# Token maxima by VectorE's 32-squares and four small transfers per pair of sequences, paired gathers, and a new hand-written order

## The chip, the cores and the metric

The kernel runs on one core of a Trainium2 chip. The core has five engines that run side by side, each through its own list of instructions in order: TensorE (PE; its weight loads are shown as PEld), VectorE (DVE), ScalarE (ACT), GpSimd (POOL) and SyncE (SP), which here only issues DMA transfers. The engines wait for one another through semaphores. The metric is the device time in microseconds; a figure given as "the time" is the median of three runs. A profile is one separate execution with the hardware profiler on.

## The reference

Eight sequences x of 256 tokens by 128 features in float32 run through a block of this kind: a mixture-of-slots layer (soft MoE), linear attention with 16 heads, the same mixture-of-slots layer a second time, a gated feed-forward layer with ternary weights, random-feature attention (FAVOR), and the feed-forward layer again, each added to x. The change touches the mixture-of-slots layer:

```python
logits = einsum('bnd,esd->bnes', x, se)          # 256 tokens x 1024 slots per sequence
dispatch = softmax(logits, axis=1)               # over tokens
combine = softmax(logits.reshape(b, n, -1), -1)  # over all 1024 slots of a token
slots = einsum('bnd,bnes->besd', x, dispatch)
eout = expert_e(slots)                           # 16 experts, 64 slots each
out = einsum('bns,bso->bno', combine, eout)
```

The softmax of `combine` subtracts from each token's logits their maximum over all 1024 slots: the token maxima of the title.

## The kernel before

**Stages.** The eight sequences form two groups of four. Each group goes through two mixture layers (with linear attention, `linear`, between), a feed-forward stage (`glu`), FAVOR attention (`favor`) and a second `glu`. The functions of a stage only record steps: for each, the engines that could run it with a planned cost, what it reads and writes, and the buffers it takes. All are recorded first, then `Plan.place` puts them in the sequence of the tuple `ORDER`, a hand-made list of step numbers (a negative number takes a step's second possible engine), gives each a planned start, and hands out buffers of the pools in `kinds`. `Plan.issue` emits the steps sorted by planned start. So stages of different groups lie in between one another, and each engine's list is fixed by `ORDER`. Where a TensorE step that takes a new PSUM bank is planned to wait over 700 ns, `issue` puts filling products against the identity ahead of it (`idle`, line L1440 before and L1503 after), which keep TensorE's clock up and compute nothing.

**`dispatch(b, sl, late)`**, per sequence and layer: normalize x (`norm`; statistics on VectorE, the root on GpSimd), transpose it by identity products (`transposed`), write the normalized tokens to DRAM and read them back four times over, so that each group of 32 partitions holds all tokens (`replicated`). Then eight matmuls of logits (L670), 128 slots by 256 tokens each, copied from PSUM into the buffer `comb` (128 partitions x 8 x 256). A partition holds a slot of each of eight blocks. For the softmax over tokens, per half of `comb`: maxima (L701), exponentials with sums (L709), reciprocals (L717), a multiplication on GpSimd (L722) into `ex`, and a VectorE transposition of 32x32 squares (L730). The gather (`gathered`, L743) multiplies the squares with the replicated tokens in 32 matmuls on quarters of the array, and four evacuations with the affine scale (`affinely`, L560 or L562) put the slots into `sl`.

**The token maxima.** Within a partition, the maximum over the eight slot blocks is taken on VectorE: in the very first layer (`late`) in one reduction (L762), else while the logits are copied (L687) and by a last `fold` (L759). Then it has to go across the 128 partitions. Before the change:

```python
flip(pt.ap[:, t, :], pm.ap[:, 0, ts(t, P)])       # transpose by identity: tokens on partitions
nc.vector.tensor_reduce(mn.ap, pt.ap, AX.X, ALU.max)
flip(pb.ap[:, ts(t, P)], mn.ap[:, t : t + 1].to_broadcast([P, P]))  # back, on all partitions
```

`flip` is line L455 in the profile, the reduction L778; a copy from PSUM (`evacuated`, L460 or L462) gives `mb`. GpSimd subtracts `mb` from `comb` (L796) and ScalarE takes the exponentials (L802).

**`experts`** loads the weights of one expert after the other (L823, six buffers), multiplies (L837), applies GELU on ScalarE (L843) and the gate on VectorE (L848), multiplies again (L868), adds the bias (L874) and places the result by transfer (L881). **`combine`** (L910) multiplies the exponentials with the experts' results. In `glu`, L1193 and L1196 are the two gates, L1124 the hidden products, L1138 and L1109 their sums, L1146 the GELU and L1221 the last product. L519 and L525 are the transfers of another transposition through DRAM (`squares_turned`).

Of the kernel before, what the change touches and what calls it, by code (L numbers as in the profile page):

```python
# [9 lines left out]
F32 = mybir.dt.float32  # L10
# [3 lines left out]
P = 128  # L14

ORDER = (
    10, 11, 0, 37, 38, 3, 19, 20, 1, 2, 7, 8, 6, 4, 5, 13, 12, 40, 39, 41, 43, 53, 44, 42, 21, 22,
    23, 24, 14, 132, 133, -136, 172, 62, 63, 31, 134, 136, 137, 15, 16, 17, 18, 142, 140, 60, 9,
    143, 141, 32, 25, 26, -34, -35, 35, 36, 56, 1329, -28, 92, -29, 93, -96, -95, 98, 61, 173,
    1286, 1287, 148, -1290, 149, 29, -31, 68, 138, -1289, 146, 147, 57, 144, -146, 96, 97, 69,  # L20
    150, 66, 67, 64, 65, 163, 1292, 100, 73, -175, 104, 105, 70, 101, 102, 103, 106, 107, 164,
    139, -176, 176, 108, 1290, 177, 182, -1292, 180, 1294, 1330, -1332, -1333, 1333, 165, 166, 71,
    74, 178, 153, 109, 1334, 75, 76, 186, 187, 181, 184, 167, 72, 113, 114, 151, 183, 1345, 77,
    99, 154, 78, 82, 79, 80, 185, 81, 110, 1302, 1339, 51, 1295, 1337, 1338, 83, 115, 1342, 111,
    112, 116, 188, 155, 156, 117, 118, 193, 1335, 1336, 189, 1340, 152, 50, 1341, 190, 191, 194,
    119, 157, -123, 1343, 179, -121, 195, 1344, 1347, 121, 1346, 196, 192, 197, 158, 1299, 1348,
    160, 159, 162, 49, 161, 1349, 168, 48, 355, 203, 198, 200, -202, -200, 1372, 1296, 204, 1415,
    84, 85, 205, 202, 359, 366, 370, 1416, -1419, 1297, 1298, 1301, 1303, 360, 361, 356, 1304,
    357, 358, 1373, -1375, 250, 251, 252, 253, 1375, 1350, 1351, 254, 324, 325, 326, 1300, 328,
    334, 1353, 1376, 1377, 1310, 1305, 367, 379, 86, 368, 87, 88, 369, 206, -1418, 373, 338, 335,  # L30
    374, 219, 255, 256, 268, 90, 329, 371, 330, 372, 376, 327, 269, 1382, -208, 210, 341, 123,
    342, 1388, 339, 340, 336, 337, 1380, 1363, 1306, 1381, 170, 1384, 377, 220, 1307, 124, 125,
    -1390, 52, 345, 1385, 1354, 1355, 261, 223, 352, 353, 221, -1384, 224, 1387, 1378, 1356, 346,
    1386, 1320, 349, 350, 292, 293, 262, 225, 222, 347, 263, 1293, 1390, 1406, 236, 237, 296, 297,
    351, 1352, 265, 266, 281, 348, 264, 294, 1407, 1408, 240, 244, 1308, 241, 295, 242, 1409, 245,
    267, 47, 1357, 303, 298, 246, 304, 305, 306, 362, 363, 307, 308, 270, 1358, 243, 208, 209,
    1396, 310, 1421, 375, 1391, -1361, 378, 1311, 311, 278, 279, 1392, 1393, 1321, 1322, -1411,
    1411, 1312, 354, 257, 258, -1362, 1397, 271, 272, 1364, 273, 309, 274, 1365, 212, 213, 214,
    216, 275, 276, 229, 230, 231, 1398, 215, 233, 282, 1313, 286, 234, 235, 1362, 313, 217, 218,
    283, 317, 323, 1394, 1379, 232, 312, 287, 314, 1359, 364, 288, 238, 284, 277, 1419, 318, 319,  # L40
    285, 315, 316, 280, 1399, 1400, 1395, 259, 344, 1413, 1323, 1324, 169, 320, 321, 1420, 1366,
    343, 289, 290, 226, 227, 228, 91, -1368, 291, 1422, 126, 127, 130, 331, 131, 1309, 1412, 239,
    1370, 247, 1314, 248, 299, 1368, 332, 333, 1325, 260, 211, 1401, 1402, 171, 300, 1369, 249,
    1315, -1319, -1320, 301, 1316, 322, 1612, 1428, 1429, 1431, 1432, 89, 1538, -1404, 1439, 1423,
    1425, -1405, 1440, -1427, 1441, -1318, 365, 302, 1496, 459, 1424, 1434, 1427, 1435, 1436,
    1326, 381, 128, 45, 380, 382, 1442, 129, 1443, 433, 1437, 1528, 1438, 1327, 1430, 383, 384,
    432, 458, 434, 1517, 435, 1433, -386, 460, 461, 386, 1444, 1549, 1446, 436, 1448, 406, -1448,
    387, 1328, 388, -438, 407, 389, -439, 462, 463, 1405, 464, 1445, 1518, 408, 465, 1449, 439,
    1542, 1543, 1616, 1613, 1614, 409, 410, 412, 411, 1544, 1497, 1498, 1500, 1501, 1499, 1519,
    1520, 1539, 1540, 1617, 1521, 1529, 1550, 1551, 1553, 1541, 1615, 442, 1618, 440, 413, 1502,  # L50
    1514, 1530, 1554, 1555, 1552, 1515, 466, 1450, 1451, 1532, 1522, 1523, 441, 443, 445, 1452,
    1531, 391, 1533, 414, 1535, 416, 468, 1453, 1454, 1371, 1536, 467, 446, 1622, 1623, 444, 449,
    448, 469, 470, 1534, 1548, 1458, 474, 1456, 471, 472, 473, 1459, 392, 397, -397, 475, 1556,
    1566, 447, 393, 394, 395, 1507, 1567, 1537, 1511, 1512, 1513, 1508, 1509, 1510, 1460, 1461,
    1465, 1469, 1557, 390, 476, 477, 398, 1470, 1471, 46, 1466, 1467, 450, 415, 399, 417, 451,
    1468, 1601, 1414, 1569, 1591, 478, 400, 401, 1524, 1525, 479, 1545, 1546, 402, 419, 1462, 403,
    404, 405, 418, 422, 1568, 484, 485, 1475, 1516, 480, 420, 421, 1595, 423, 1596, 452, 453,
    1605, 1606, 1482, 1483, -488, 1547, 454, 1479, 1602, 486, 1597, -456, 1463, 1486, 1607, 1490,
    1558, 1464, 1603, -482, 456, 1604, 488, 457, 570, 571, 1487, 1488, 489, 573, 1472, 1473, 1476,
    1477, 482, 1478, 1625, 483, 613, 614, 1580, 1584, 1585, 1491, 54, 55, 1492, 492, 494, -494,  # L60
    496, 1506, -616, 497, -499, 495, 500, 501, -617, 617, 618, 424, 425, 1592, 426, 1581, 1611,
    1480, 1489, 499, -573, 1503, 1481, 1593, 1594, 502, 1582, 1583, 1457, 508, 574, 1608, 621,
    509, 626, 1609, 622, -576, 578, 1455, 427, 623, 503, 1504, 619, 629, 624, 518, 1559, 1563,
    510, -580, 1586, 1570, 1474, 490, 625, 491, 627, 628, 631, 632, 504, 505, 1527, 580, 1610,
    582, 583, 584, 511, 512, 1598, 1624, 1599, 1493, 1494, 1495, 519, 520, 630, 581, 1564, 1560,
    1561, 1562, 428, 1565, 506, 507, 1571, 1572, 429, 1619, 1620, 1485, 1574, 1575, 1576, 1577,
    430, 431, 527, 528, 1505, 1621, 633, 513, 1578, 1573, 1587, 529, 530, 531, 532, 637, 634, 635,
    638, 1484, -516, 1588, 589, 586, 537, -588, 585, 588, 535, 594, 540, 543, -545, 536, 541, 539,
    542, 514, 1579, 636, 1590, 1600, 1526, 1589, 1653, 639, 1652, 640, 521, 620, 576, 577, 1678,
    538, 546, 545, 551, 595, 596, 641, 1679, 597, 590, 591, 592, 552, 1680, 1654, 1655, 1656,  # L70
    -1658, 598, 1627, 553, 1626, 1628, 522, 547, 533, 548, -517, 517, 642, 644, 646, 593, 599,
    -1659, 643, 1659, -646, 549, 550, 554, 561, 555, 600, 534, 556, 559, 1629, 604, 558, 1660,
    -604, 1630, -1632, 1632, 557, 1662, 1705, 1633, 1681, 1682, -1685, 1704, 1706, 562, 563, 602,
    1707, 1708, 673, 799, -1684, 560, 601, 677, 678, 679, 1634, 674, 675, 803, 804, 805, 647, 800,
    810, 778, 782, 1661, -1710, 1710, 1711, 779, 1714, 726, 801, 802, 780, 1685, 676, 811, 812,
    648, 649, 684, 783, 784, 814, 815, 1664, -1669, 1669, 816, 813, 1635, 691, 688, 689, 820, 692,
    1637, 1639, 1638, 1712, 1686, 525, 821, 690, 781, 685, 686, 687, 1663, 1665, 1713, 1642, 1643,
    789, 1715, 1717, 564, -566, 1687, 1640, 1641, 701, 702, 796, 1644, 817, 1645, 1646, 1666,
    1667, 566, 567, 730, 797, 1647, 58, 1689, 1691, 1648, 1649, 1716, 1721, -1721, 818, 568, 1690,
    757, 1695, 1718, 1719, 1670, 1671, 523, 1692, 656, 660, -1695, 657, 1693, 1636, 1722, 1723,  # L80
    1672, 1673, 661, 727, 1724, 1725, 1688, 1650, 728, 729, 736, 1651, 790, 731, 732, 761, 650,
    651, 1696, 662, 1726, 1730, 743, 744, 762, 763, 1727, 663, 667, 791, 693, 1728, 1729, 668,
    669, 605, 1674, 1675, 704, 1731, 1697, -1734, 606, 793, -1733, 1734, 664, 683, 658, -1736,
    1859, 1860, 822, 1676, -1863, 1698, 1677, 1773, 1774, 652, 794, 795, 1699, 1746, 659, 792,
    1747, 1738, 1740, 1739, 1742, 1743, 1745, 665, 806, 705, 709, 1748, 703, 809, 666, 1700, 1701,
    807, 710, 737, 1744, 1754, 819, 607, 1741, 1749, 1702, 1703, 608, -1777, 738, 758, 759, 760,
    -1776, 706, -1862, 1865, 1863, -1865, 707, 740, 739, 680, 711, 681, 1869, 708, 741, 775, 776,
    654, 1867, 1750, 798, 1868, 768, 823, -1871, 1878, 1751, 1777, 569, 1779, 1875, 670, 671,
# [1436 lines left out]
```

## Time and profile before

| what | value |
|---|---|
| time, median of 3 (lowest to highest) | 718.74 us (718.47 to 719.14) |
| the profiled execution's own time | 720.09 us |
| its span, first to last instruction | 718.4 us |
| granted TensorE clock | 1.0 over the whole span |
| transfers | 72.76 MB, 36% of 16 engines' time on the queue of SyncE |

The page of a profile gives for each engine its busy time, its share of the span and its number of instructions; the chain of work that ended last, followed back from the end; and the costliest groups of instructions, as "line engine operation out<-in shapes xcount | busy us, mean ns of one | idle time ahead and what ended it". A matmul in float32 runs as two passes and counts as two instructions in the profile. Other views are answers of the trace: busy time by stretches of the span, what an engine waited for ("engine line waited <- releaser: us in total, times, longest"), the timeline of an engine, and the chain in order of time. An engine's line number is that of the kernel, so the same line has different numbers before and after.

### The profile page before, as it was taken

The numbers are of one execution on the slowest core, as the hardware profiler recorded it, in microseconds if no ns is written. First come the engines' busy times: TensorE is split into PE (matmuls) and PEld (weight loads), VectorE is DVE, ScalarE is ACT, GpSimd is POOL, SyncE is SP. The second block draws the span as 40 slices with busy tenths as digits, with TensorE's granted clock in tenths as the row PEclk, the third lists the DMA queues.
The fourth block names the chain that finished last, engine by engine and source line by source line (L and its number), as shares of the span: only waits on it lengthen the run. The fifth ranks groups of instructions, "written<-read, shape, count | busy, mean of one in ns | idle before, by whom it ended". The sixth has DMA issues, their size and how long they took to land.

```text
span 718.4 us, 14349 instructions
## 1 busy us (share of the span) xinstructions
PE 710.3 (99%) x5266; PEld 609.3 (85%) x5266; DVE 496.6 (69%) x1087; ACT 391.4 (54%) x780; POOL 326.6 (45%) x432
## 2 busy tenths in 40 slices
PE   8999999999999999999999999999999999999998
PEld 6889889998899999999788879876886878868787
DVE  7999774767997688974534545787576877875432
ACT  4987677464865547784642544566435542452421
POOL 6848377531327355745884321352425563413020
PEclk9999999999999999999999999999999999999999
DMA  4553566154344644462642321023404143241001
GB/s 134 162 201 99 165 160 225 34 157 124 118 113 134 182 133 127 120 195 90 203 137 67 84 67 43 18 61 89 73 16 89 44 92 58 59 90 30 12 11 37
DMA packets 118741, 72.76 MB, mean 101 GB/s; under 512 B 73360, under 2 KB 107536, under 8 KB 118672
## 3 DMA queue, kind: packets, MB, share of 16 engines
q1 hardware_dynamic: 118672, 71.85, 36.0%
q8 instruction: 42, 0.69, 0.4%
q14 instruction: 27, 0.22, 0.1%
HBM read 51.89 MB, written 11.53 MB: 88 GB/s over the span
## 4 chain that ended last, share of the span: by engine, by line
PE 95%; POOL 2%; DMA 1%; ACT 1%; DVE 1%; issue 0%; POOLq 0%; ACTq 0%
PE ps L1124 27%; PE ps L837 15%; PE ps L743 8%; PE ps L910 8%; PE ps L868 7%; PE ps L670 7%; PE ps L1221 4%; PE ps L1193 4%; PE ps L1196 4%; PE ps L455 2%; PE ps L1297 1%; PE ps L1347 1%; PE ps L1382 1%; PE ps L958 1%; DMA we<-in_We 1%; POOL sm L486 1%
## 5 line engine op out<-in xcount | busy, mean ns | idle before, releaser
L837 PE MATMUL ps<-slots,we 128*128 128x256 f32 x512 | 122.5, 380 | 1.8 <-ACT k L843 0.9
L837 PEld LDWEIGHTS ps<-slots,we 128*128 128x128 f32 x512 | 92.9, 190 | 14.8 <-ACT slots L560 1.2
L1124 PE MATMUL ps<-comb,comb 128*128 128x256 f32 x448 | 103.0, 380 | 0.0
L1124 PE MATMUL ps<-comb,slots 128*128 128x256 f32 x448 | 102.5, 380 | 0.0
L1124 PEld LDWEIGHTS ps<-comb,slots 128*128 128x128 f32 x448 | 84.1, 190 | 13.2 <-issue 1.8
L1124 PEld LDWEIGHTS ps<-comb,comb 128*128 128x128 f32 x448 | 83.6, 190 | 13.1 <-issue 1.7
L843 ACT ACTIVATE k<-ps,small 128x256 f32<-128x256 f32 x128 | 57.5, 475 | 60.1 <-PE ps L837 52.5
L796 POOL TENSOR_TENSOR comb<-comb,k 128x1024 f32<-128x1024 f32 x32 | 75.4, 2364 | 31.3 <-ACT k L460 8.8
L722 POOL TENSOR_TENSOR comb<-comb,sm 128x1024 f32<-128x1024 f32 x32 | 60.3, 1895 | 41.5 <-DVE sm L717 37.8
L848 DVE SCALAR_TENSOR_TENSOR k<-ps,small,k 128x256 f32<-128x256 f32 x128 | 57.4, 476 | 19.5 <-ACT k L843 18.2
L460 ACT COPY k<-ps 128x512 f32<-128x512 f32 (+2 forms) x52 | 25.6, 497 | 78.9 <-PE ps L1124 56.1
L868 PEld LDWEIGHTS ps<-we,k 128*128 128x128 f32 x512 | 63.6, 192 | 4.8 <-issue 2.0
L709 ACT ACTIVATE comb<-comb,sm 128x256 f32<-128x256 f32 x128 | 63.6, 507 | 4.6 <-DVE sm L701 2.4
L868 PE MATMUL ps<-we,k 128*128 128x128 f32 x512 | 65.7, 276 | 0.0
L484 POOL TENSOR_SCALAR sm<-sm 128x2 f32<-128x2 f32 x52 | 10.0, 193 | 121.7 <-DVE sm L478 112.1
L1138 DVE TENSOR_TENSOR comb<-ps,k 128x512 f32<-128x512 f32 x48 | 32.6, 686 | 47.1 <-PE ps L1124 35.3
L670 PE MATMUL ps<-k,seT 128*128 128x256 f32 x256 | 60.4, 383 | 0.8 <-ACT seT L596 0.4
L910 PEld LDWEIGHTS ps<-slots,comb 128*128 128x128 f32 x512 | 58.6, 192 | 1.3 <-issue 1.0
L910 PE MATMUL ps<-slots,comb 128*128 128x129 f32 x512 | 59.6, 276 | 0.0
L743 PE MATMUL ps<-comb,k 32*128 32x256 f32 x1024 | 59.5, 379 | 0.0
L1146 ACT ACTIVATE comb<-comb 128x512 f32<-128x512 f32 x48 | 29.3, 629 | 51.9 <-DVE comb L1138 51.8
L743 PEld LDWEIGHTS ps<-comb,k 32*128 32x128 f32 x1024 | 52.7, 185 | 4.5 <-ACT comb L460 0.3
(147 smaller groups left out, 1286.0 us busy)
## 6 DMA issues: line engine op xcount, KB each, us to landing
we<-in_We SPq DMA_DIRECT2D x64, 448.0 KB, 4.1
k<-y SPq DMA_DIRECT2D x64, 128.0 KB, 2.7
slots<-k SPq DMA_DIRECT2D x128, 64.0 KB, 2.1
t<-comb SPq DMA_DIRECT2D x8, 512.0 KB, 2.8
k<-t SPq DMA_DIRECT2D x32, 128.0 KB, 3.1
y<-k SPq DMA_DIRECT2D x16, 128.0 KB, 2.6
t<-k SPq DMA_DIRECT2D x16, 128.0 KB, 1.7
k<-t SPq DMA_DIRECT2D x64, 32.0 KB, 2.3
```

The costliest lines, as they stand in the source:

```text
L670: mm(pl.ap[:, j, :], seT[:, 2 * u + j].rearrange("p k s -> p (k s)"), yt.ap, start=True, stop=True,)
L709: nc.scalar.activation(ex.ap[:, 4 * h + j, :], comb.ap[:, 4 * h + j, :], AF.Exp, bias=mx.ap[:, j : j + 1], accum_out=mx.ap[:, 4 + j : 5 + j],)
L722: return nc.gpsimd.tensor_tensor(ex.ap[:, part], ex.ap[:, part], mx.ap[:, 8:12].unsqueeze(2).to_broadcast([P, 4, N]), ALU.mult,)
L743: mm(po.ap, yr.ap[rows, TT * (c % 4) + c // 4, :], ex.ap[rows, :, 32 * c : 32 * c + 32], start=(c == 0), stop=(c == N // 32 - 1), tile_pos ...
L796: return nc.gpsimd.tensor_tensor(raw, raw, mb.ap.unsqueeze(1).to_broadcast([P, 4, N]), ALU.subtract)
L837: mm(pe.ap[:, m, :], we.ap[:, ts(2 * m + c, P)], sl.ap[:, j, k, :, 0:S], start=True, stop=True,)
L843: nc.scalar.activation(ga.ap, pe.ap[:, 0, :], AF.Gelu, bias=bg[:, e, c : c + 1])
L848: nc.vector.scalar_tensor_tensor(ht.ap[:, c, :], pe.ap[:, 1, :], bu[:, e, c : c + 1], ga.ap, ALU.add, ALU.mult,)
L868: mm(po.ap[:, r, :], ht.ap[:, c, ts(r, P)], we.ap[:, ts(4 + c, P)], start=(c == 0), stop=(c == 1),)
L910: mm(po.ap[:, t, 0 : D + 1], comb.ap[:, j, ts(t, P)], eo()[:, j, q, 0 : D + 1], start=(j == 0), stop=(j == NJ - 1),)
L1124: mm(bank.ap[:, o], w(k)[:, c, ts(o, P)], rhs().rearrange("p (c n) -> p c n", c=2)[:, c, :], start=(start and o + c == 0), stop=(stop and ...
L1138: nc.vector.tensor_tensor(C(i, k)(), bank.ap.rearrange("p o n -> p (o n)"), other(), ALU.add)
```

## The change

`dispatch` now ends with the squares of `ex`. The gather is a function of its own and takes one or two sequences; with two, their results lie in one PSUM bank each and leave it in one evacuation of 512 columns. It takes two where the group and the layer have different numbers, one where they are equal. The token maxima are a third function, `maxima`, for two sequences always: VectorE transposes the 32x32 squares of the folded maxima and takes the maximum in each square, which leaves for each token four maxima, one for each 32 partitions; a transfer writes them to DRAM (`spill`), a second reads them back so that the four lie side by side on 32 partitions (`fetch`); VectorE takes their maximum and turns the square; a third transfer writes 512 maxima to DRAM (`give`), and a fourth reads them on all 128 partitions (`spread`). The identity products, the reduction from PSUM and the copy are gone. The pool of `comb` has ten buffers instead of nine, that of `k4` five instead of four, and the scratch memory for dynamic DMA is set to 2048 bytes. `plan.tag` is set in many places and only labels steps. `ORDER` is new throughout, so all engines' lists differ from the first instruction on.

```diff
     kinds = {
-        "comb": (NJ * N, 9),
+        "comb": (NJ * N, 10),
...
-        "k4": (1024, 4),
+        "k4": (1024, 5),
...
+        return comb, pm, ex, yr
+
+    def gather(b, got, sl):
+        n, q = len(got), b % BG
+        pos = [ps_(n, NJ, 32) for _ in range(4)]
         def gathered(_):
-            for c in range(N // 32):
-                for a, po in enumerate(pos):
...
+            for k, (_, _, ex, yr) in enumerate(got):
+                for c in range(N // 32):
+                    for a, po in enumerate(pos):
+                        rows = slice(32 * a, 32 * a + 32)
+                        mm(po.ap[:, k], yr.ap[rows, TT * (c % 4) + c // 4, :],
+                           ex.ap[rows, :, 32 * c : 32 * c + 32], ...)
...
+    def maxima(b, got, late):
+        n = len(got)
+        mb, mq = Buf("k2", (P, n, N)), Buf("sm", (P, 32))
+        K = n * N // 32
...
-        step({"PE": flips(TT)}, turn_max, [pm], [pt])
-        step({"DVE": dve(N)}, token_max, [pt], [mn])
...
-        step({"PE": flips(TT)}, spread, [mn], [pb], takes=[mb])
-        evacuated(lambda: mb.ap, lambda: pb.ap, [pb], [mb], N)
+        def quarters(_):
+            nc.vector.transpose(flat(), flat())
             nc.vector.tensor_reduce(
+                mq.ap[:, 0:K], flat().rearrange("p (k j) -> p k j", j=32), AX.X, ALU.max)
+        def spill(_):
+            nc.sync.dma_start(parts.rearrange("a i k -> (a i) k"), mq.ap[:, 0:K])
+        def fetch(_):
+            nc.sync.dma_start(flat()[0:32, 0 : 4 * K].rearrange("i (a k) -> i a k", a=4),
+                              parts.rearrange("a i k -> i a k"))
+        def tops_of(_):
+            four = flat()[0:32, 0 : 4 * K].rearrange("i (a k) -> i k a", a=4)
+            nc.vector.tensor_reduce(
+                mq.ap[0:32].rearrange("i (r k) -> i r k", k=K),
+                four.unsqueeze(1).to_broadcast([32, 32 // K, K, 4]), AX.X, ALU.max)
+            nc.vector.transpose(flat()[0:32, 4 * K : 4 * K + 32], mq.ap[0:32])
+        def give(_):
+            nc.sync.dma_start(whole, flat()[0:K, 4 * K : 4 * K + 32])
         def spread(_):
-            for t in range(TT):
-                flip(pb.ap[:, ts(t, P)], mn.ap[:, t : t + 1].to_broadcast([P, P]))
+            nc.sync.dma_start(flat(), whole.rearrange("k i -> (k i)").partition_broadcast(P))
...
+            first, single = g + layer == 0, g == layer
+            for b in bs_ if single else bs_[::2]:
+                got = []
+                for k in range(1 if single else 2):
+                    got.append(dispatch(b + k, sl, first))
+                if single:
+                    both.append((b, got[0]))
+                gather(b, got, sl)
+                if single and len(both) == 2:
+                    got = [z for _, z in both]
+                    b, both = both[0][0], []
+                if len(got) == 2:
+                    maxima(b, got, first)
```

## The prediction

> **What bounds the kernel now.** First the page: the busy share of each engine, and the engines' shares of the chain that ended last.
>
> ```profile
> PE 710.3 (99%) x5266; PEld 609.3 (85%) x5266; DVE 496.6 (69%) x1087; ACT 391.4 (54%) x780; POOL 326.6 (45%) x432
> ...
> PE 95%; POOL 2%; DMA 1%; ACT 1%; DVE 1%; issue 0%; POOLq 0%; ACTq 0%
> ```
>
> TensorE (PE) is busy 710.3 of 718.4 us and carries 95% of the chain. A busy share alone doesn't say that an engine is full. So, second, the busy time of TensorE in two stretches, cut where the experts' products begin (columns: stretch, its length, busy time), and, third, all that TensorE waits for after the cut.
>
> ```profile
> 0.00:52.50 52.50, 49.37 (x430) 1.00 0.54 170
> 52.50:718.40 665.90, 660.95 (x4838) 1.00 0.35 96
> ...
> PE ps L837 <- ACT k L843: 0.9, 1, 0.9
> PE ps L837 <- DMA we<-in_We: 0.6, 1, 0.6
> PE ps L837 <- DVE k L874: 0.3, 1, 0.3
> ```
>
> After 52.5 us it idles 4.95 us. Of this 3.1 are the tail behind its last product, which ends at 715.3; 1.85 are waits, in 663 us. There, a product taken from TensorE's list is worth the time it occupies, and work put on other engines costs nothing until something arrives late. The first 52 us differ. The timeline of TensorE, then of VectorE (DVE), shows why (start, length, instruction):
>
> ```profile
> 30.04 3.92 PE L743 MATMUL ps<-comb,k 32*128 32x256 f32 x64
> ...
> 28.62 1.25 DVE L730 STREAM_TRANSPOSE comb<-comb 128x1024 f32<-128x1024 f32 x1
> 47.55 3.77 DVE L762 TENSOR_REDUCE k<-comb 128x256 f32<-128x2048 f32 x1
> 51.30 0.99 DVE L562 TENSOR_SCALAR slots<-ps,small 128x256 f32<-128x256 f32 x2
> ```
>
> The first gather (L743) starts at 30.04, 0.17 us after the end of the VectorE transpose that it needs. The first expert product comes at 52.55, just after the last slots leave PSUM (52.29), and these stood behind a maximum of 3.77 us (L762). VectorE sets the pace there.
>
> **What is removed.** Per sequence and layer two transposes of maxima and two spreading products against the identity go: 4 x 16 = 64, from 144 identity products to 80. Two views give a price, that of the line's durations and the chain in order of time:
>
> ```profile
> L455 PE MATMUL ps<-ident,sm x32: 272/273/273, 27.1 to 342.6; 128*128 128x128 f32 x32
> ...
> 27.08 0.44 PE ps L455 x4
> ```
>
> Each lasts 273 ns, but four take 0.44 us of the chain, 0.11 each, because neighbours overlap. 64 x 0.11 = 7.0 us. The Trainium skill (TensorE: Matmul & The Clock Gate, Part 4: PE-mode transpose) puts one at about 275 ns in a kernel's context, which is this row's duration; priced so, the removal would be an estimated 17.6 us, and the spacing in the chain speaks against that.
>
> VectorE loses 16 reductions L778 of 0.41 us (6.6 us), ScalarE (ACT) 15 copies of 0.38 us (5.7 us). Hardly anything on TensorE waited for them: zero.
>
> **The gathers.** The same 512 matmuls remain; pairing saves the seam between two gathers. The chain again:
>
> ```profile
> 47.55 3.67 PE ps L743 x64
> ...
> 106.08 7.12 PE ps L743 x128
> ```
>
> Two in a row take 7.12, not 2 x 3.67: 0.22 us per seam. But the old order already has neighbours: its 16 gathers stand in 11 runs. The new order has 10. Gain 0.2 us. The evacuations fall from 64 to 48, the paired ones twice as wide; other stages' products follow each paired gather and cover them.
>
> **What is added on VectorE.** Per pair: a transpose of 512 columns (L516, 0.71 us); a maximum of 512 to 16 (nearest L1309, 0.68); a small maximum over 128 elements (between L611's 0.17 and L778's 0.41; I take 0.25); a transpose of one square (between 0.18 for the smallest statistics row and 0.44 for 256 columns; I take 0.2, as it is nearer in size). Together 1.84 us, for eight pairs 14.7, net of L778 8 us: from 69% to about 70%. Behind them in VectorE's queue stand evacuations, and TensorE waits for those. But after 52.5 us VectorE has 47 blocks of 1.2 us (L730, L701) and one of 3.77 in the same queue, and the waits are those shown. So zero, at 1.4 us for each block whose cover is gone. The skill (VectorE: DVE Perf Modes, Rules for kernel authors) speaks against the change: it sends a 128x128 transpose to TensorE where PSUM will do. By that rule the sum would have no gain and an estimated 8 us of extra VectorE work; the busy shares above say that here TensorE is the engine to spare.
>
> **What is added on SyncE (SP).** 32 transfers, per pair four in series: spill, fetch, give, spread. Nearest rows of the transfers (last number: us from issue to landing):
>
> ```profile
> t<-k SPq DMA_DIRECT2D x16, 128.0 KB, 1.7
> k<-t SPq DMA_DIRECT2D x64, 32.0 KB, 2.3
> k<-t SPq DMA_DIRECT2D x32, 128.0 KB, 3.1
> ```
>
> Four are between 6.8 and 12.4 us. The first three move 8 KB or less, the last writes 256 KB: I take 1.7 + 2.1 + 1.7 + 2.8 = 8.3. With VectorE's 1.84 the maxima take 10 us instead of about 2. The cover is the experts: the maxima serve GpSimd's (POOL) subtraction L796 (four of 2.36 us per pair), ScalarE's exponentials (1.06) and only then the combining product L910, behind all sixteen experts. A stage of experts is (122.5 + 65.7) / 4 = 47 us of TensorE by lines L837 and L868. 10 + 9.5 + 1 fits.
>
> Fetch and spread wait on SP for a landing, the experts' weights (L823) queued behind them. SP has taken such waits (L525 for its spill: 22.8 us over 16, 1.9 at most), and TensorE waited 0.6 us for weights in all. Zero; 1 to 3 us for each that breaks through.
>
> ScalarE's list has 71 table loads instead of 57: 14 x 1.28 = 18 us, less 5.7. Zero by the same argument, 1.28 for each that stands in front of an activation TensorE needs. Pools, scratch size and tags issue nothing.
>
> **The new start.** Up to the first expert product TensorE's list has 22 identity products instead of 28, the same logits and gathers, and 35 filling products instead of 25. VectorE's list now has two maxima L762 ahead of the first gather's last transpose, where one stood. The statistics block ends 1.1 us later (two more pairs, one more normalization); then come seven maxima L701 (1.1 each), two L762 (3.67), three reciprocals (0.08) and two transposes (1.14): 14.3 + 1.1 + 17.6 = 33.0. TensorE's list agrees: eight more logits (0.44 each) and two more fills, less four identity products, put 30.04 at 33.6. By VectorE the second gather is ready at 39.3 (L762, two transposes), the third at 43.4, the fourth at 48.7. A gather takes 3.67, so the fourth ends at 52.4; the slots take 1.4 more, as before: 53.8, or +1.25 us. Bounds: 0, if the early waits shrink; +3, if each of three gaps costs a further half microsecond.
>
> **Sum.** After the first expert product 116 identity products become 58: 58 x 0.11 = 6.4 less; the seam 0.2 less; the start 1.25 more. Net -5.35: the span goes from 718.4 to 713.05. The profiled execution's own time was 720.09, 1.69 over its span, so 714.74; it stood 1.35 over the median of 718.74, so the median goes to 713.4. The 1.85 us of waits I leave. They can go (-1.85) or, since every queue is ordered anew, grow: four more like the longest (0.9) are +3.6. So the forecast's own range is 711.5 to 717.0.
>
> **Rivals.** *The chain of transfers arrives late* (slower). Its weakest place is the last pair of the second group's second layer: its fetch stands 24 issues behind its spill on SP, eight fetches of hidden weights among them (4.4 to 4.7 us to landing), its spread another 24 on. If the cover is gone, the price is what the chain adds, 8 us: 721.4. It turns the sign once the last exponential ends over 5.3 us after TensorE is ready for that product. Against it: nine of the sixteen experts' placements still follow the spread, some 9 x 2.9 = 26 us of TensorE, for 2.8 + 9.5 + 1. *VectorE or ScalarE takes it back* (no change): 8 and 12 us more work, and a quarter of it (5 us) in front of evacuations gives 718.4. For it: the first 52 us, where VectorE is the bound. Against: from 130 to 230 us it is busy 80%, later less. *A denser order*: the waits go and the start costs nothing, 713.4 - 1.85 - 1.25 = 710.3. That nothing is removed is excluded: the instruction lists show the 64 gone.
>
> **Chances.** Forecast 0.72; denser order 0.05; no change, 717.0 to 720.2, 0.09, of which 0.01 still below 717.3; late chain, or a wait of that size elsewhere, 0.14. A measurement of this kernel tells 0.2%, 1.4 us, from no change: faster is below 717.3, slower above 720.2. Faster 0.78, same 0.08, slower 0.14. The range 711.0 to 720.0 leaves out the late chain and most of the denser order, under 0.2.
>
> **What would show it.** Right: about 7 us less identity work on TensorE and 2 us more fills; double gathers of 7.1 us; the first expert product near 53.8; waits of TensorE after it under 5 us; the spread landing long before L910. Wrong: TensorE waiting at L910 for ScalarE's exponentials (late chain), waits for evacuations over all stages (the engines), or a first expert product after 56.

## The result and the profile after

The changed kernel takes 721.05 us (median of 13 runs, 719.88 to 724.78), the kernel before 718.74 (13 runs, 717.71 to 719.83). The ratio is 1.0038, 95% interval 1.0027 to 1.0049: 2.7 us (1.9 to 3.5) slower. The forecast of 713.4 us and its range, 711.0 to 720.0, missed it. The profiled execution took 722.52 us, 1.47 over the median. Differences of two experiments below are taken from their ratios to the kernel before, times 718.7 us; their error is the two half intervals added in squares.

The page after, with the lines shown of before:

```profile
PE 707.7 (98%) x5222; PEld 607.4 (84%) x5222; DVE 504.3 (70%) x1098; ACT 394.6 (55%) x755; POOL 335.9 (47%) x444
...
PE 77%; DVE 8%; DMA 6%; SPq 3%; ACT 3%; POOL 1%; issue 1%; DVEq 0%; ACTq 0%
```

TensorE is 2.6 us less busy in a span 2.4 us longer, and its share of the chain falls from 95% to 77%: VectorE, transfers and SP's own queue (SPq) now stand in it. Where, the stretches tell, cut at the first expert product and at the first combining product (length, then each engine's busy time, clock, share of the DMA engines, GB/s). After:

```profile
0.00:54.80 54.80, 50.72 (x444) 43.94 (x445) 48.82 (x92) 41.12 (x119) 33.75 (x68) 1.00 0.50 152
54.80:118.70 63.90, 59.45 (x420) 52.61 (x418) 47.93 (x97) 42.64 (x97) 36.74 (x29) 0.97 0.55 147
118.70:720.80 602.10, 597.51 (x4360) 510.87 (x4360) 407.52 (x910) 310.89 (x542) 265.41 (x347) 1.00 0.36 95
```

Before, cut at the same two products:

```profile
52.50:116.70 64.20, 63.34 (x507) 56.34 (x506) 49.24 (x100) 47.95 (x103) 43.04 (x35) 1.00 0.49 136
116.70:718.40 601.70, 597.61 (x4333) 511.15 (x4331) 400.59 (x898) 303.93 (x562) 248.27 (x331) 1.00 0.34 92
```

The start is 2.3 us longer. The middle stretch, the first stage of experts (group 0, layer 0), holds 87 TensorE instructions fewer (22 of them identity products, which are one instruction each; 64 of a gather that moved behind it) and ends only 0.3 us shorter: TensorE idles 4.45 us in it, 0.86 before, and its mean clock is 0.97. What it waited for, over the whole span:

```profile
PE ps L878 <- DMA we<-in_We: 3.8, 5, 2.1
PE ps L952 <- DMA slots<-k: 1.9, 1, 1.9
```

First the weights of the experts (`We`, in the buffers `we`; L878 reads what L864 loads). SP's timeline:

```profile
84.99 0.54 SPq L864 DMA_DIRECT2D we<-in_We  x1
85.57 0.45 SPq L819 DMA_DIRECT2D k<-m  x1
86.12 0.38 SPq L864 DMA_DIRECT2D we<-in_We  x1
```

TensorE's timeline:

```profile
86.84 4.48 PE L878 MATMUL ps<-slots,we 128*128 128x256 f32 x20
93.42 1.84 PE L878 MATMUL ps<-slots,we 128*128 128x256 f32 x4 [2.10 <-DMA we<-in_We]
```

The load issued at 86.12 stands behind a spread (L819, 256 KB) and lands 7.17 us later, at 93.29, as the chain in order of time has it; the one of 84.99 took 3.19.

```profile
86.12 7.17 DMA we<-in_We
```

TensorE waits 2.1 us, and then:

```profile
90.00:93.40 3.40, 1.32 (x7) 0.82 (x6) 3.37 (x7) 1.57 (x5) 3.40 (x4) 1.00 1.02 285
93.40:95.00 1.60, 1.57 (x4) 1.31 (x5) 1.17 (x3) 0.00 (x0) 1.60 (x2) 0.57 0.89 264
95.00:97.00 2.00, 2.00 (x10) 1.94 (x9) 0.48 (x1) 0.47 (x1) 2.00 (x1) 0.50 0.27 75
```

The granted clock (third number from the end) falls to half, from 93.64 to 97.05 us by the trace; 0.57 is the mean of a stretch that begins before the fall. Half of 3.41 us, another 1.7 us, is lost. That belongs to the traced execution and not to the median one: such a fall lowers the mean clock of the whole span by 0.0024, and the mean clock is 0.998 or less in three of the thirteen runs (722.52, the traced one, 723.39 and 724.78 us) and 0.999 or more in the other ten. Second, the wait at L952. SP's timeline:

```profile
99.73 1.24 SPq L922 DMA_DIRECT2D slots<-k  x2
101.02 0.59 SPq L816 DMA_DIRECT2D m<-k  x1
101.65 3.95 SPq L922 DMA_DIRECT2D slots<-k  x6
105.70 1.34 SPq L819 DMA_DIRECT2D k<-m  x1
107.09 10.08 SPq L922 DMA_DIRECT2D slots<-k  x14
```

TensorE's:

```profile
118.74 1.47 PE L952 MATMUL ps<-slots,comb 128*128 128x129 f32 x11 [1.87 <-DMA slots<-k]
```

22 transfers (L922, the placements of eleven expert outputs, two each) leave SP one behind the other at about 0.7 us each, with a give and a spread (together 2.0 us) among them, and the last one's landing at 118.6 releases the combining product. SP had stood still before:

```profile
SPq L922 <- PE ps L878: 8.0, 1, 8.0
```

From 91.70 to 99.70 it waited at one placement for a hidden product; ten others were queued behind it.

### The profile page after: what moved, and what is told of

Same layout as the page of the kernel before. It is cut to its first block, busy times and chain, and to the rows that moved or that the text cites. A ratio compares the mean times of both kernels' runs of the same rounds, so it can differ in the third digit from the quotient of the medians.

```text
span 720.8 us, 14235 instructions
## 1 busy us (share of the span) xinstructions
PE 707.7 (98%) x5222; PEld 607.4 (84%) x5222; DVE 504.3 (70%) x1098; ACT 394.6 (55%) x755; POOL 335.9 (47%) x444
## 4 chain that ended last, share of the span: by engine, by line
PE 77%; DVE 8%; DMA 6%; SPq 3%; ACT 3%; POOL 1%; issue 1%; DVEq 0%; ACTq 0%
PE ps L1167 26%; PE ps L878 12%; PE ps L952 6%; PE ps L909 6%; DMA we<-in_We 5%; PE ps L749 4%; PE ps L1265 4%; PE ps L1237 4%; PE ps L1240 4%; PE ps L670 3%; DVE sm L701 2%; SPq L922 2%; DVE k L783 2%; DVE comb L730 1%; PE ps L1342 1%
## 5 line engine op out<-in xcount | busy, mean ns | idle before, releaser
L878 PE MATMUL ps<-slots,we 128*128 128x256 f32 x512 | 122.5, 383 | 4.0 <-DMA we<-in_We 3.8
L878 PEld LDWEIGHTS ps<-slots,we 128*128 128x128 f32 x512 | 94.5, 191 | 19.3 <-issue 5.4
L1167 PE MATMUL ps<-comb,slots 128*128 128x256 f32 x448 | 104.7, 381 | 0.0
L889 DVE SCALAR_TENSOR_TENSOR k<-ps,small,k 128x256 f32<-128x256 f32 x128 | 57.0, 474 | 36.4 <-ACT k L884 33.7
L709 ACT ACTIVATE comb<-comb,sm 128x256 f32<-128x256 f32 x128 | 63.5, 512 | 4.6 <-DVE sm L701 4.6
L952 PEld LDWEIGHTS ps<-slots,comb 128*128 128x128 f32 x512 | 58.1, 192 | 3.7 <-POOL comb L722 2.2
L952 PE MATMUL ps<-slots,comb 128*128 128x129 f32 x512 | 59.1, 276 | 1.9 <-DMA slots<-k 1.9
L749 PE MATMUL ps<-comb,k 32*128 32x256 f32 x1024 | 58.7, 378 | 0.2 <-DVE comb L730 0.2
L1152 POOL TENSOR_TENSOR comb<-comb 128x512 f32<-128x512 f32 x24 | 30.4, 1272 | 57.1 <-DVE comb L1152 20.6
L670 PEld LDWEIGHTS ps<-k,seT 128*128 128x128 f32 x256 | 46.6, 190 | 8.7 <-ACT seT L593 1.8
```

Of the source, the lines that this page charges most:

```text
L670: mm(pl.ap[:, j, :], seT[:, 2 * u + j].rearrange("p k s -> p (k s)"), yt.ap, start=True, stop=True,)
L709: nc.scalar.activation(ex.ap[:, 4 * h + j, :], comb.ap[:, 4 * h + j, :], AF.Exp, bias=mx.ap[:, j : j + 1], accum_out=mx.ap[:, 4 + j : 5 + j],)
L749: mm(po.ap[:, k], yr.ap[rows, TT * (c % 4) + c // 4, :], ex.ap[rows, :, 32 * c : 32 * c + 32], start=(c == 0), stop=(c == N // 32 - 1), ti ...
L878: mm(pe.ap[:, m, :], we.ap[:, ts(2 * m + c, P)], sl.ap[:, j, k, :, 0:S], start=True, stop=True,)
L889: nc.vector.scalar_tensor_tensor(ht.ap[:, c, :], pe.ap[:, 1, :], bu[:, e, c : c + 1], ga.ap, ALU.add, ALU.mult,)
L952: mm(po.ap[:, t, 0 : D + 1], comb.ap[:, j, ts(t, P)], eo()[:, j, q, 0 : D + 1], start=(j == 0), stop=(j == NJ - 1),)
```

## The experiments

*Theory 1:* the new transfers hold up We loads and placements in the first stage of experts. *Rivals:* the new order does it whatever the transfers are; VectorE's new work does it. The start is a question of its own.

**Without the transfers.**

```diff
-            nc.sync.dma_start(parts.rearrange("a i k -> (a i) k"), mq.ap[:, 0:K])
+            pass
... (the same for fetch, give and spread)
-                    nc.scalar.activation(raw, raw, AF.Exp)
+                    nc.scalar.activation(raw, raw, AF.Exp, scale=0.001)
```

> The changed kernel, its order kept, without the four transfers of each pair (spill, fetch, give, spread: 32 in all), so that the token maxima stay unfinished; the exponentials are scaled so that they stay finite. Line theory: the transfers stand in SP's line and in the DMA engines ahead of We loads and of the transfers that put expert outputs in place, and so cause the waits of the first expert stage (2.3 us at L878 near 91 us, 2.0 us at L952 near 117 us, and the halved clock of 93.4 to 97 us, 1.9 us). Without them these go: first expert product still near 54.8, PE's waits at L878 and L952 under 1.5 us in sum, total 714 to 716.5 us. Rival, the order: the new order drives the ring of six We buffers too hard and puts 22 place transfers at the end of the stage whatever else SP does: the waits stay above 3.5 us, total 719.5 or more. Rival, VectorE: its added transposes and reductions hold up the bias additions that free We: the same, 719.5 or more.

717.38 us, ratio 0.9974 (0.9962 to 0.9986): 4.6 us (±1.2) less than the changed kernel and the forecast of theory 1 missed by a little. First expert product at 54.96, first combining product at 113.47 (118.74 in the changed kernel). What is left of the two waits:

```profile
PE ps L873 <- DMA we<-in_We: 2.2, 3, 1.3
PE ps L947 <- DMA slots<-k: 1.0, 1, 1.0
```

(L873 and L947 are L878 and L952.) The We waits of the first stage are gone, the longest now stands in the next and ends at 154 us; the placements' wait is half there. So the transfers cost more than the whole loss of 2.7 us, and what is left of the wait at L947 is there without them.

**Line or bytes?**

```diff
-                flat(), whole.rearrange("k i -> (k i)").partition_broadcast(P)
+                flat()[0:1], whole.rearrange("k i -> (k i)").partition_broadcast(1)
```

> The changed kernel with the spread L819 to one partition in place of 128 (2 KB in place of 256 KB each; maxima wrong, the exponentials scaled so that they stay finite): the 32 transfers keep their issues and waits in SP's line, but 2 MB of DMA work go. If the line is what costs (issues of 0.4 to 1.3 us and waits for landings): total 720 to 721.5, stage waits as before. If the bytes in the DMA engines cost: the We landing of 7.2 us near 86 us falls to 4 to 5 us, the wait at L878 near 91 us and the halved clock go, and the total is near that without transfers, 717 to 718.5.

717.73 us, 0.9991 (0.9982 to 0.9999): 3.4 us (±1.0) less, with every issue and wait of SP's line still there. The stretch from 70 to 85 us of the changed kernel, then of this run:

```profile
70.00:85.00 15.00, 14.48 (x87) 13.13 (x86) 11.99 (x29) 11.10 (x30) 8.84 (x9) 1.00 0.87 217
```

```profile
70.00:85.00 15.00, 15.00 (x90) 13.64 (x89) 12.71 (x29) 11.69 (x32) 10.24 (x10) 1.00 0.74 209
```

The DMA engines go from 0.87 to 0.74 busy and TensorE has no idle time. The median landing of a We load (last number) falls as well, from the first line to the second:

```profile
we<-in_We SPq DMA_DIRECT2D x64, 448.0 KB, 4.9
```

```profile
we<-in_We SPq DMA_DIRECT2D x64, 448.0 KB, 4.4
```

So of the four transfers it is mostly the 256 KB of the spread that cost, and not their place in SP's queue: leaving out all four saves 1.2 us (±1.1) more than leaving out the spread's bytes.

**The transfers on another engine's queue.** `nc.sync` becomes `nc.gpsimd` in one run, `nc.scalar` in the other.

> The changed kernel with the same 32 transfers issued by GpSimd in place of SP, all work kept. Line theory: SP's line is free of them, so the wait at L952 near 117 us (2.0 us) goes, as the give and the spread held SP for 2.0 us there; the wait at L878 near 91 us shrinks only in part, because the 256 KB of the spread still go through the same DMA engines: 715 to 718.5 us. If the DMA engines' load alone counts, 720 to 721. If GpSimd's waits for the transfers hold up its own subtractions and norms, slower than 721, with PE waits behind L722 or L481.

> The changed kernel with the 32 transfers issued by ScalarE in place of SP, all work kept. GpSimd's issue put 13 us on the time, as its subtractions and norms stood behind each transfer's wait. ScalarE is busy 55 percent but evacuates TensorE's results and makes the gelus: if its waits for landings (1.5 to 4 us, three a pair) hold those up, 724 to 735, with TensorE waits behind L884, L457 and L557; if it is mostly idle where they stand, SP's line gets shorter by about 1 us a pair and the total is 718 to 720.

734.47 us, 1.0217 (1.0199 to 1.0235), and 731.74 us, 1.0174 (1.0156 to 1.0193). Both are slower, in the ranges expected for an engine whose own work is held up. Freeing SP's line buys nothing: on GpSimd, TensorE waits 2.0 us near 97 us, now for VectorE's gate (L889), and 1.6 us at L952, now for a GpSimd instruction (L927). The waits for landings now hold up what the other engine does. GpSimd at its subtraction, and TensorE behind ScalarE's evacuations in the other run:

```profile
77.25 2.35 POOL L837 TENSOR_TENSOR comb<-comb,k 128x1024 f32<-128x1024 f32 x1 [4.42 <-DMA k<-m]
```

```profile
PE ps L1029 <- ACT slots L557: 5.1, 1, 5.1
```

**The order of the placements.**

```diff
 ORDER = ( ... 276,
+    360, 308, 266,
 ... 234, ...
-    308, ... 266, ... 360, ...
```

> The changed kernel with all its work; in the order of steps alone, three placements of expert outputs of group 0, layer 0 (steps 360, 308 and 266, six transfers, L922) stand before step 234, where SP waited 8.0 us for a hidden product, in place of behind it. Order theory: the wait of 2.0 us at L952 near 117 us is the end of SP's row of placements at 0.65 us an issue; six issues fewer behind the wait are 3.9 us, so the wait goes and the total falls by 1.5 to 2.1 us, to 719 to 719.6. Rival: the row is not what ends last (landing of We or the exponentials come next), the wait stays over 1 us under another name, total 720.3 or more.

718.76 us, 1.0009 (0.9997 to 1.0020): 2.1 us (±1.1) less, as the order theory had it. The first combining product comes at 114.39, straight behind the logits ahead of it:

```profile
110.84 3.72 PE L670 MATMUL ps<-k,seT 128*128 128x256 f32 x16
114.39 1.84 PE L952 MATMUL ps<-slots,comb 128*128 128x129 f32 x15
```

So the wait at L952 goes with the order alone: SP took ten placements late because the one in front was not ready.

**The spreads behind the We loads.**

```diff
 ORDER = (as place_order)
+    299, 199, ...            # a We load, then the spread it stood behind
-    199, ... 299, ...
+    267, ... 208, 309, 121,  # three We loads, then the other spread
-    121, ... 267, ... 208, 309,
```

> The changed kernel with all its work; in the order of steps the three early placements as in the run place_order, and the two spreads of group 0, layer 0 (steps 199 and 121, L819, 256 KB each) behind the We loads that they stood ahead of: load 299 before spread 199, spread 121 after loads 267, 208 and 309. Bytes theory: a We load that SP issues behind a spread lands late by its 256 KB, so the landings of 5.5 us near 72 us and of 7.2 us near 86 us fall to about 4.5 and 5.5, the waits at L878 near 77 and 91 us (0.8 and 1.5 us in the run place_order) fall under 0.6 us in sum: total 716 to 717.5, faster than the kernel before. Rival: the first stage's DMA engines are full whatever the order (0.87 busy from 70 to 85 us), the waits only move to the next We load or behind the subtractions: 718.3 to 719.5, as place_order.

718.34 us, 0.9996 (0.9987 to 1.0005): 0.9 us (±1.1) less than place_order, which decides nothing. The landings did what was expected, 3.4 us instead of 5.5 near 72 us and 4.3 instead of 7.2 near 86; the waits for We fell to

```profile
PE ps L878 <- DMA we<-in_We: 2.4, 3, 1.0
```

over the span (4.3 in place_order), but a wait of 0.9 us for VectorE came up at L878. This is the best version with all its work: faster than the change, not to be told from the kernel before.

**Do the two costs add up?** no_transfers with the order of place_order:

> The run no_transfers with the three early placements of place_order, work left out as there. If the two costs of the first expert stage are separate they add up: the wait of 1.2 us at L947 (the combine) that no_transfers still had goes too, 715.8 to 716.6. If they are one, 717 to 717.8, as no_transfers.

716.29 us, 0.9974 (0.9962 to 0.9985), the same ratio as no_transfers. The traces show the wait at the combine gone (first combining product at 112.50 instead of 113.47), the ratios no gain (0 ± 1.2 us). Not settled; the two prices overlap at least in part.

**VectorE's part.**

```diff
-            nc.vector.transpose(flat(), flat())
...
-                mq.ap[:, 0:K], flat().rearrange("p (k j) -> p k j", j=32), AX.X, ALU.max
+                mq.ap[:, 0:K], flat().rearrange("p (k j) -> p k j", j=32)[:, :, 0:2], AX.X, ALU.max
```

> The changed kernel with its 32 transfers, but without VectorE's transposes L793 and with the reductions L794 over 32 columns in place of 512 (maxima wrong, the exponentials scaled so that they stay finite): about 1.3 us of VectorE less for each of eight pairs, 10 us in all. The run exchange_on_vector, with about 1 us more a pair, one copy of 2.06 us among them, took 5 us more than the changed kernel. If VectorE's additions cost as well as the spread's bytes: 717.5 to 719.5, with smaller waits for We, as L915 frees it earlier. If they are off the path, as the prediction had it: 720.3 to 721.8.

720.47 us, 1.0034 (1.0017 to 1.0052): 0.3 us (±1.5) less, the changed kernel's time for about 9.7 us less VectorE work. VectorE's additions were off the path, as predicted.

**VectorE in place of the spread.** Without the 256 KB: the fetch goes to all partitions, VectorE repeats the maxima and turns them.

```diff
-            nc.vector.transpose(flat()[0:32, 4 * K : 4 * K + 32], mq.ap[0:32])
+            nc.vector.tensor_reduce(mq.ap[:, 0:K], four, AX.X, ALU.max)
+            nc.vector.tensor_copy(
+                flat().rearrange("i (k j) -> i k j", j=32),
+                mq.ap[:, 0:K].unsqueeze(2).to_broadcast([P, K, 32]),
+            )
+            nc.vector.transpose(flat(), flat())
... (give and spread left out)
```

> The changed kernel, its order kept, with all its work: the fetch brings the quarter maxima to all 128 partitions (32 KB in place of 8), and VectorE ends the exchange itself (a reduction to 16 columns, a copy that repeats each 32 times, a transpose of 32-squares of 512 columns), so that the give and the spread are left out: 2 MB of DMA work and 16 of SP's issues less, about 1.2 us of VectorE more for each of eight pairs. Bytes theory: as the run small_spread, whose work was incomplete, the waits at L878 of the first expert stage shrink to under 1 us and the total is 717 to 718.5. Rival: VectorE is by then the engine that holds We's release (63 to 70 percent busy, 90 in the first stage), and 8 to 10 us more on it give the time back: 720 or more.

> exchange_on_vector with the three early placements of place_order. If the two costs of the first expert stage are separate (bytes ahead of We, 3 us; SP's row of placements, 2 us), both go: 715.5 to 717, faster than both kernels. If they are one (the late We load makes the placements late as well), it ends where exchange_on_vector or place_order do: 717.5 to 719.

725.91 us, 1.0105 (1.0091 to 1.0118), and 725.70 us, 1.0098 (1.0083 to 1.0114): 4.8 us (±1.2) slower than the change, as the first run's rival had it, although the waits for We did fall (1.4 us over the span, 3.8 in the change). The second run misses both of its ranges: the order can't help then. TensorE's longest wait is for a bias addition (L914), and in VectorE's list a copy that took five times its usual length stands ahead of that (first the copy's line in the trace, with its shortest, median and longest duration in ns):

```profile
L810 DVE COPY k<-sm x8: 426/428/2061, 65.3 to 380.9; 128x512 f32<-128x512 f32 x8
```

GpSimd's and VectorE's timeline at the longest:

```profile
88.89 1.89 POOL L722 TENSOR_TENSOR comb<-comb,sm 128x1024 f32<-128x1024 f32 x1 [2.11 <-DVE sm L717]
89.00 2.06 DVE L810 COPY k<-sm 128x512 f32<-128x512 f32 x1
```

and TensorE's longest wait (L877 is L878 of the change):

```profile
PE ps L877 <- DVE k L914: 2.1, 1, 2.1
```

**The price of the identity products**, in the kernel before: left out, and done twice.

```diff
-            for t in range(TT):
-                flip(pt.ap[:, t, :], pm.ap[:, 0, ts(t, P)])
+            pass                                  # first run; `spread` likewise
+            for t in (*range(TT), *range(TT)):    # second run; `spread` likewise
+                flip(pt.ap[:, t, :], pm.ap[:, 0, ts(t, P)])
```

> The kernel before, without the 64 identity products of the token maxima (the reductions and copies behind them read what is there; the exponentials are scaled so that they stay finite). This prices the term that the prediction subtracted: 64 times 0.11 us is 7.0 us, and with the 0.5 us wait for the first norm untouched the time should be 711 to 712.5 us. At their full length of 273 ns each it would be 701 to 702 us; if the products lie in waits that something else sets, 716 or more.

> The kernel before with each of the 64 identity products of the token maxima done twice: 64 more at 0.11 us, 7.0 us. Taking them out gave 4.0 us and not 7.0. If products lie on TensorE's path and their removal only brought other waits out, adding gives the full price: 725 to 726.5. If part of them lies in waits of TensorE that are there anyway, adding costs as little as removing gave: 722 to 723.5.

715.04 us, 0.9946 (0.9933 to 0.9958): 3.9 us less (3.0 to 4.8). 724.34 us, 1.0083 (1.0071 to 1.0095): 6.0 us more (5.1 to 6.8). By the pages TensorE is 5.0 us less busy without the 64 products and 6.0 us busier with 64 more (710.3 us before), so that one takes 0.08 to 0.09 us of its time and not 0.11:

```profile
PE 705.3 (99%) x5202; PEld 604.1 (85%) x5202; DVE 497.6 (70%) x1087; ACT 390.9 (55%) x780; POOL 326.6 (46%) x432
```

```profile
PE 716.3 (99%) x5330; PEld 616.4 (85%) x5330; DVE 496.8 (69%) x1087; ACT 391.8 (54%) x780; POOL 325.9 (45%) x432
```

In the second of these traces all of TensorE's waits after the first expert product are gone. Whether taking the products away brings waits out is not settled: TensorE idles 8.0 us without them and 8.1 in the trace of before, but that execution is 1.35 us above its kernel's median. Without the products the first four gathers start at 29.92, 37.54, 42.30 and 47.48 us, within 0.12 of before, and the first expert product at 52.39 (52.55): the start does not notice its own products.

**The start.** Three runs: the late maximum L783 over two of eight blocks (`comb.ap[:, 0:2]`); no fills (`if s.idle > 700 and False`); no fills and one activation of 1024 columns for L709 in the first layer.

> The changed kernel with the late maximum L783 of group 0, layer 0 over two of eight slot blocks (wrong maxima; the exponentials are scaled so that they stay finite): four instructions of 3.76 us become about 1 us each. VectorE theory of the start: the chain of the first 50 us is VectorE's (L783, L701, L730), so the first expert product comes from 54.8 to 51 to 52.5 us and the total falls by 2 to 3.5 us, to 717.5 to 719. Rival, TensorE sets the start, with its 35 filling products and its logits: the first expert product stays within 0.5 us of 54.8 and the total at 720 to 721.5.

> The changed kernel without the filling products inside the program (the 14 at its start stay): 42 matmul records fewer, 0.112 us each, 4.7 us. As the run with the short late maximum left the first expert product at 55.1 us, TensorE and not VectorE sets the start. If the fills lie on the path: first expert product at 50.5 to 52.5 us, total 717 to 719. If they lie in waits that something else ends (affine evacuations, key tiles, the replicated tokens): first expert product within 0.7 us of 54.8, TensorE waits in their place, total 720 to 722, and a lower granted clock there if the waits are long.

> The run no_fills with the slot exponentials L709 of group 0, layer 0 as one activation of 1024 columns per half instead of four of 256 with sums (their sums are left out, so the weights are wrong): ScalarE has about 1 us less work in each of eight halves. In no_fills the first expert product came at 56.6 us, behind a chain of L709 and L457 on ScalarE. If ScalarE sets the start: first expert product at 50 to 53.5 us and total 715 to 718.5. If VectorE's transposes and maxima set it as well: 55 to 56.6 us, total 720 or more.

First expert product at 55.09, 56.63 and 54.81 us (54.81 in the changed kernel); times 723.68 (1.0059, 1.0039 to 1.0078), 721.75 (1.0043, 1.0030 to 1.0057) and 722.91 (1.0069, 1.0050 to 1.0089). In none of the three do both numbers fall in one of its forecasts. L783 does not set the start alone, and the fills stand where TensorE would wait anyway. Without them, TensorE's timeline:

```profile
33.74 4.07 PE L749 MATMUL ps<-comb,k 32*128 32x256 f32 x64 [1.15 <-ACT comb L709]
39.81 5.81 PE L749 MATMUL ps<-comb,k 32*128 32x256 f32 x66 [2.00 <-ACT slots L557]
```

and the stretch of the second of these lines, with its clock:

```profile
39.80:46.00 6.20, 5.81 (x66) 5.42 (x66) 4.66 (x8) 4.32 (x18) 4.45 (x3) 0.72 1.00 390
```

The second gather waits until ScalarE has emptied the first one's banks, and the clock falls (to half from 40.28 to 43.69 us; 0.72 is the mean of the stretch): the fills save the 1.8 us that their absence costs in the start; in the total it is 0.4 us (±1.3). Shorter exponentials bring the start back by 1.8 us, no more. Both runs with less work in the start end no earlier than the changed kernel, 1.5 (±1.6) and 2.2 us (±1.6) later, and their traces have more waits for We (7.3 us over the span with the short maximum, 3.8 in the changed kernel). Why that is so stays open.

**A filled wait.** Nine filling products ahead of the hidden product that waited:

```diff
+            if s.run.__name__ == "hidden":
+                count += 1
+                if count == 27:
+                    idle(s.bank, 9)
             made = s.run(s.engine)
```

> The changed kernel with nine filling products (18 records of 0.112 us, 2.0 us) on TensorE ahead of the hidden product that waited 2.3 us for We near 91 us. If the halved granted clock from 93.4 to 97 us is set off by that idle time, it stays at 1.00 there and the run saves up to 1.9 us where the wait is full and loses up to 2.0 where it is short: total 719.5 to 721, with less spread between runs. If the clock falls for another reason, it falls here too, and the total is 721 to 723.

722.14 us, 1.0051 (1.0039 to 1.0063). The trace:

```profile
93.40:97.00 3.60, 3.60 (x25) 3.23 (x24) 2.76 (x6) 0.47 (x1) 3.60 (x3) 1.00 0.78 228
```

The clock held, in all five runs (mean 0.999 or more), but the time, 0.9 us (±1.2) above the changed kernel's, is in the range of the rival. So fills hold the clock where that wait would let it fall; as it falls in three of the changed kernel's thirteen runs only, they save nothing in the median.

## Why the prediction was wrong

**The step that failed: transfers priced at zero.** "Zero; 1 to 3 us for each that breaks through" was said of waits in SP's queue, and the cover looked at was the one for the maxima themselves. That cover held: in the changed kernel's trace TensorE never waits at L952 for an exponential. But the chain's last member also occupies the DMA engines, and in the first stage of experts We loads have little room: in the trace of before the last five loads of that stage land 0.1 to 2 us ahead of their use. The spread's 2 MB cost 3.4 us (±1.0, small_spread), all 32 transfers 4.6 (±1.2, no_transfers). The four took 2.4 + 2.9 + 2.0 + 4.8 = 12.1 us in series by the median landings, where 8.3 was predicted:

```profile
k<-m SPq DMA_DIRECT2D x8, 256.0 KB, 4.8
...
q<-sm SPq DMA_DIRECT2D x8, 8.0 KB, 2.4
k<-q SPq DMA_DIRECT2D x8, 8.0 KB, 2.9
m<-k SPq DMA_DIRECT2D x8, 2.0 KB, 2.0
```

**The order, taken as given.** The prediction left before's 1.85 us of waits and allowed +3.6 "since every queue is ordered anew", without looking for the weak places in SP's list. One was there to be seen: a placement that needs the hidden products of two experts, with ten others behind it. It cost 2.1 us (±1.1, place_order) with the transfers in place.

**The removed products: right in count, mis-sized in effect.** 144 became 80. The term of -6.4 us measured -3.9 (3.0 to 4.8) when the same products, and six more in the start, were taken out of the kernel before. Part of that is the price of one: 0.11 us was read from four products in a row, and over all 64 it is 0.08 us of TensorE's busy time when they go and 0.09 when they are doubled. The rest, 1.1 us, is about the size of the error; that it turns into waits is not shown. The other price weighed there, 17.6 us, is far from both.

**The start: +2.3 us instead of +1.25**, within its bounds of 0 and +3. The first gather came at 33.82 (33.0 to 33.6 predicted; at 0.11 us for a fill or an identity product the sum over TensorE's list gives 33.3, not 33.6), the fourth at 49.77 (48.7). "VectorE sets the pace there" is not shown: short_late_max and short_exps_no_fills moved little. In the new list the eight matmuls of logits that stood between the first two gathers (3.72 us) stand ahead of the first one, so that TensorE has only fills while that gather's banks are emptied; that this is the cause is argued from the lists, no run moved the logits.

**Right.** VectorE's additions measured 1.93 us a pair (1.84 predicted), and leaving out 9.7 of their 15.5 us saved 0.3 us (±1.5, no_quarters). TensorE waited for no table load. Two gathers in a row take 7.12 us; all gathers together occupy TensorE for 58.7 us instead of 59.5, and how much of that is the 0.2 us of the seam no run tells.

**The sum, mended:** -3.9 (products) + 4.6 (transfers) + 2.3 (start) = +3.0 us; measured +2.7 (1.9 to 3.5). Without the transfers it is -1.6, and no_transfers measured -1.9 (±0.9): even with the transfers free, the forecast gain of 5.35 us would not have come. The first two terms have errors of about 1 us each, the third is a reading of two traces, and what the larger pools and the scratch size do no run tells by itself. The order of the placements is not added as a fourth term: without the transfers it no longer shows in the ratio. Of the rivals, the late chain named the right cause, transfers, but a wrong place: not the last pair of maxima being late for L952, but the first stage's weights and placements late behind them. That its 721.4 us is so near is luck: it adds 8 us for a lost cover to the forecast, and the cover was not lost.

## What to carry to other kernels

A transfer that is itself in good time still has a price: look at which transfers are issued within some microseconds behind it and how much time those have in hand, in bytes per stretch and not only in waits of the queue. Price removed work from both sides: take it out and double it, as the two can differ (here 3.9 and 6.0 us for the same products). And read a queue that works in order for its first instruction that isn't ready: what stands behind it, ready, can be had by order alone (here 2.1 us).

## What was not expected of the hardware

A wait of about 2 us can halve TensorE's granted clock, and whether it does depends on where it lies. In the traces that hold the changes of the clock (all but that of spread_behind_we) each one stands a whole number of steps of 3.41 us behind its first rise (88.75 us or 26 steps in the changed kernel, 34.13 or ten in no_fills, 259.41 or 76 in transfers_on_gpsimd), and a fall within the program lasts one step, or two after the wait of 5.1 us in transfers_on_scalar. A fall came behind each step at full clock with 1.98 us or more of idle time on TensorE (1.98 in transfers_on_gpsimd, 2.00 in no_fills, 2.10 in the changed kernel), and behind none with 1.90 or less. A wait of 2.05 us that lay across two steps (short_exps_no_fills, 1.29 us of it in the first) left the clock at 1.00, and so did the 1.9 us wait at L952. The Trainium skill (TensorE: Matmul & The Clock Gate, Part 1: The HAM clock gate) puts the fall at one idle window of about 3.4 us. The length is that of the step seen here; but in the changed kernel TensorE was busy for 1.3 us of the step before the fall, so less than a whole idle window was enough. No run varied the idle time on purpose.

A VectorE copy of 512 columns (L810 in exchange_on_vector) took 2.06 us instead of 0.43 and ended at 91.06, 0.28 us after the GpSimd multiplication that had begun 0.11 us before it. A second, of 1.68 us, ended 0.28 us after another such multiplication too; the other six, with none beside them, took 0.43 to 0.53. The skill (SBUF — State Buffer, SBUF: two separate sides) describes it: some VectorE instructions share a port pair with GpSimd, and whichever comes second is blocked for the other's whole length. The trace agrees.
